# Two state-space layers on one core: where layer 1's near part and tail put their loads, sums and roots

## The chip, the cores and the metric

One core of one Trainium2 chip. Its engines are TensorE (PE: matmuls), VectorE (DVE), ScalarE (ACT), GpSimd (POOL) and SyncE (SP). Each takes its own instructions in order, and they wait for one another by semaphores. TensorE writes to PSUM, the other on-chip memory is SBUF. Transfers between these and the main memory are issued by SP, ScalarE or GpSimd, each on a queue of its own, and carried by 16 DMA engines that all queues share. The metric is the device time of one launch in microseconds (us), the median of several runs.

## The reference, cut to what matters

An image of 64 x 64 tokens with 96 channels goes through two layers of the same build: group norm, projection to 192 channels and as many gates, depthwise 3x3 convolution, four scans along rows and columns in both directions, layer norm, gating, projection back, and the sum with the input.

```python
# one layer (both have these steps; what differs is the form of the scan)
xz = gn(x) @ in_proj_w
xin, z = split(xz)
u = silu(depthwise_conv3x3(xin) + conv_b)
dt = softplus((u @ x_proj)[:6] @ dt_proj + bias)   # B, C: 16 states each
# per channel and state n, along each of four orders of the tokens
h[t] = h[t-1] * exp(dt[t] * A[n]) + dt[t] * u[t] * B[t, n]
y[t] = sum_n h[t, n] * C[t, n] + u[t] * D
y = layernorm(y1 + y2 + y3 + y4) * g + b
x = x + (y * silu(z)) @ out_proj_w
```

Layer 1 computes its scan as `decay * cumsum(dB_u / (decay + 1e-12))`: once the decay has fallen far enough under 1e-12, a state gives nothing any more. So all that its scans give lies near their starts. Layer 2's scans are true recurrences over all 4,096 tokens.

## The kernel before

Channels lie on partitions: 192 channels as three blocks T = 0, 1, 2 of 64, each block with the two halves of the image on partitions 0 to 63 and 64 to 127, so that a tensor like `u[T]` or `y[T]` is 128 x 2048. A chunk c (0 to 3) is 512 of these columns. Many operations are recorded by one helper, so that their line in the profile is L271 (the class `Ordered`, which keeps an engine's instructions in the order of the program) or L805 (the same within layer 2's scans); the names of their tiles tell them apart.

Layer l runs: `head` (norm of the group, projection `in`, convolution with `pad`, gates `sz` stored to `szd`), the scans, `tail` or `last_tail`.

**Layer 1's near part, `near_scans`.** Only the first 192 steps of each of four directions are computed, and fewer for the states that decay faster: `kinds` holds (192, state pair 0), (64, pair 1), (32, pairs 2 to 7). `us` is the input of the scans, 128 x 3 x 2 x 384; `dt`, `du` and `S` (the running sum of dt) have that shape too. `steps_of(T)` copies dt (ScalarE), forms du = dt times us (VectorE), sends both across the two halves of the partitions by SP (`across`) and forms the sums (VectorE). `sums_of(T)` copies the sums to `S` and sends them across. B and C, 16 rows each, are stored to main memory (`stored`) and fetched again with every row spread over 64 partitions (`fetched`). The work is cut into six units j: `operands(j)` gives the decays a, `weights_of(j)` a weight `wt` from `S` by Tanh, `inputs(j)` B times du (GpSimd), `scan(j)` the weighting product `nbw` and the scan `nnh` on VectorE and the product with C, `nnhc`, on GpSimd; `add(j)` sums over states in PSUM by matmul. `mean` and `centre` take the mean over channels off y. The order of all this is written out by hand at the end of the function; `look_ahead()` in it loads layer 2's small weights and the half p=1 of its scan weights. The function returns a flag that tells whether the near steps were enough; every engine reads it and branches over the full form (`far_scans`), which doesn't run with these inputs.

**Scan weights, `scan_weights(l, p, queue)`.** For layer 2 they are 44 loads for one p: 11 each for two directions and two halves. Before, the half p=0 is loaded by the loop over layers, on SP's queue as it is, not in the hand-written order: a scheduler places the loads where their tiles are free.

**Layer 1's tail, `tail`.** It works by chunk from 3 down to 0. `squares` (ScalarE), `variance` (matmuls with a matrix of means), `root` (Ln, then Exp with -0.5), then the gating y * root * gain + bias times the gate: blocks 0 and 1 on VectorE (`gated`, two instructions), block 2 on GpSimd and ScalarE (`pool_gated`); `project` (12 matmul records a chunk), `add` (sum with x and statistics for layer 2's norm, VectorE; a write to `xs` by SP, which only the last tail reads). `load_exp_ln()` asks for a ScalarE table that holds both Exp and Ln.

Then layer 2's `head` begins with the aggregation `gst` of the statistics, a norm with Ln and Exp, and the projections `in`; `borders(b)` copies, by SP, the border rows between the parts of `pad`, which the taps of the upper and lower row of the convolution need. Its first scan step needs the half p=0 of the scan weights.

The part of the hand-written orders that the change touches:

```python
            steps_of(0)
            inputs(0)
            inputs(1)
            steps_of(1)
            cb += [fetched("C", rows, i) for i in range(1, len(kinds))]
            sums_of(0)
            mean(3)
...
            load_exp_ln()
            squares(3)
            variance(3)
            squares(2)
            root(3)
```

Of the kernel before, what the change touches and what calls it, by code (L numbers as in the profile page):

```python
# [21 lines left out]
NS = 16  # L22
# [22 lines left out]
def two_ss2d_layers(  # L45
# [231 lines left out]
    def near_scans(weights, ds):  # L277
# [5 lines left out]
        with ExitStack() as sc:  # L283
# [42 lines left out]

            us = once.tile([128, 3, 2, 2 * NEAR], F32, name="nus")
            k = NEAR // HW
# [45 lines left out]
            def fetched(what, kept, i):  # L374

                n, m0, m1 = kinds[i]
                t = once.tile([128, m1 - m0, 4, n], F32, name=f"n{what}b{n}")
                for h, half in enumerate(HALF):
                    if n in kept:
                        to, of = t[half], kept[n][2 * m0 + h : 2 * m1 : 2]  # L380
                    else:
                        to, of = t[half, 0], kept[NEAR][2 * m0 + h, :, 0:n]
                    sp.dma_start(out=to, in_=of.unsqueeze(0).to_broadcast(to.shape))
                return t.rearrange("p n d w -> p (n d w)")

            rows = stored("B", 0)
            B = [fetched("B", rows, i) for i in range(len(kinds))]
            rows = stored("C", NC - NS)
            cb = [fetched("C", rows, 0)]

# [16 lines left out]
            for i, (n, m0, m1) in enumerate(kinds):  # L407
# [4 lines left out]
            )  # L412
            dt, du, S = (
                once.tile([128, 3, 2, 2 * NEAR], F32, name=f"n{nm}") for nm in ("dt", "du", "S")
            )
# [69 lines left out]
            def operands(j):  # L485
                T, ks = units[j]
                long = sum(4 * kinds[i][0] * (kinds[i][2] - kinds[i][1]) for i in ks)
                a, wt, h, hc = live[j] = [
                    nb.tile([128, 1024], F32, tag=nm, name=f"n{nm}{j}")[:, 0:long]
                    for nm in ("na", "nwt", "nh", "nhc")  # L490
                ]
# [126 lines left out]
            steps_of(0)  # L618
            inputs(0)
            inputs(1)  # L620
            steps_of(1)
            cb += [fetched("C", rows, i) for i in range(1, len(kinds))]
            sums_of(0)
            mean(3)
# [910 lines left out]
    def tail(l, w, xT):  # L1535
# [3 lines left out]
        with ExitStack() as sc:  # L1539
# [26 lines left out]
            def root(c):  # L1566
                r = live["r", c] = fin.tile([128, HT], F32, tag="rstd", name=f"rstd{l}_{c}")
                act.activation(r, live.pop(("v", c)), AF.Ln, bias=eps5)
                act.activation(r, r, AF.Exp, scale=-0.5)

# [4 lines left out]
            def gated(c, T):  # L1575
                q, gain, bias = result(c, T)
                dve.scalar_tensor_tensor(
                    q, y[T][:, at(c)], gain, live["r", c], ALU.mult, ALU.mult
                )
                dve.scalar_tensor_tensor(q, q, bias, sz[c, T], ALU.add, ALU.mult)  # L1580

            def pool_gated(c, T):
                q, gain, bias = result(c, T)
                pool.tensor_mul(q, y[T][:, at(c)], live["r", c])
                act.activation(q, q, AF.Identity, bias=bias, scale=gain)
# [11 lines left out]
            def add(c):  # L1597
                po = live.pop(("o", c))
                for h in range(2):
# [3 lines left out]
                    sp.dma_start(out=xs[:, at(g)], in_=xT[:, at(g)])  # L1603

            load_exp_ln()
            squares(3)
            variance(3)
            squares(2)
            root(3)
            for c in order:  # L1610
# [3 lines left out]
                for T in (0, 1):  # L1614
                    gated(c, T)
                if c > 1:
                    squares(c - 2)
                if c:
                    root(c - 1)
                project(c)  # L1620
# [171 lines left out]
    def look_ahead():  # L1792
        ahead["w"] = layer_weights(1, sp)
        ahead["sw"] = scan_weights(1, 1, sp)

    for l in range(2):

        w = ahead.pop("w") if l else layer_weights(0, nc.sync)
        sw = list(zip(*[scan_weights(l, 0, nc.sync)] + ([ahead.pop("sw")] if l else [])))

# [103 lines left out]
```

## Time and profile before

| what | value |
|---|---|
| median of 3 runs | 1483.68 us (1482.44 to 1490.68) |
| profiled execution | 1493.08 us, its span 1491.1 us |
| instructions | 17293 |
| busy share of the span | DVE 90%, ACT 83%, PE 82%, POOL 82% |
| granted TensorE clock | 0.922 of full |

The page's 40 slices are 37.3 us each. Digits are busy tenths of an engine in a slice:

```profile
PE   5864668788888888888887989888889898887988
DVE  5848578688999998999999999999998999999996
ACT  5755547789889978999999999999997999897873
POOL 2715228779989897999898989898989898989895
PEclk9986789589999989999999999999998999999999
```

Slices 3 to 6, roughly 75 to 224 us, are the near part, the tail and the start of layer 2: there no engine is near full. From about slice 8 on layer 2's scans keep VectorE nearly full up to the last slice.

In the timeline used below each line has the start in us from the span's start, the length, engine, line, operation with output and inputs, and in brackets the idle time just before and what ended it. SPq is SP issuing a transfer. In groups, the columns are operation and shapes with the count, busy us and mean ns of one, and the idle time before them by releaser.

### The profile page before, as it was taken

How to read it: one execution, taken by the hardware profiler on the slowest of the kernel's cores; microseconds unless marked ns; L12 is line 12 of the kernel's file. 1: busy time of each engine (PE TensorE's matmuls, PEld its weight loads, DVE VectorE, ACT ScalarE, POOL GpSimd, SP SyncE). 2: the span in 40 equal slices, each digit the busy share in tenths (PEclk: the TensorE clock that was granted, in tenths of full speed). 3: DMA queues.
4: the chain of work that ended last, by engine and by line, in shares of the span. 5: the costliest groups of instructions: out<-in, count | busy, mean ns of one | idle time of the engine just before them, and what ended most of it. 6: DMA issues, size and time to landing. Idle time of an engine off the chain costs nothing.

```text
span 1491.1 us, 17293 instructions
## 1 busy us (share of the span) xinstructions
PE 1225.7 (82%) x5019; PEld 471.8 (32%) x5019; DVE 1338.8 (90%) x920; ACT 1234.6 (83%) x2524; POOL 1220.4 (82%) x678
## 2 busy tenths in 40 slices
PE   5864668788888888888887989888889898887988
PEld 2233213333332323233333333333333332322333
DVE  5848578688999998999999999999998999999996
ACT  5755547789889978999999999999997999897873
POOL 2715228779989897999898989898989898989895
PEclk9986789589999989999999999999998999999999
DMA  3241522515252625262626262626262626262634
GB/s 106 73 120 30 141 50 84 140 45 137 63 133 63 149 57 128 62 149 62 153 60 145 57 143 58 142 58 142 59 141 59 142 59 147 62 146 62 151 84 129
DMA packets 87475, 148.65 MB, mean 100 GB/s; under 512 B 34572, under 2 KB 38476, under 8 KB 87276
## 3 DMA queue, kind: packets, MB, share of 16 engines
q1 hardware_dynamic: 85692, 144.92, 40.4%
q0 software_dynamic: 576, 1.57, 0.5%
q10 hardware_dynamic: 1104, 0.98, 0.2%
q8 instruction: 40, 0.66, 0.2%
q14 instruction: 63, 0.52, 0.1%
HBM read 81.77 MB, written 12.17 MB: 63 GB/s over the span
## 4 chain that ended last, share of the span: by engine, by line
DVE 23%; issue 19%; PE 14%; ACT 13%; POOL 8%; DMA 8%; SPq 5%; DVEq 0%; POOLq 0%; ACTq 0%
DVE h L805 15%; DVE b L805 6%; POOL hc L805 5%; DMA cb<-C 4%; ACT a L805 4%; PE pj L805 4%; SPq L805 3%; ACT bT L805 3%; PE ys L805 3%; PE b L805 2%; DMA dt<-sp 2%; DMA szt<-szd 1%; POOL sp L805 1%; PE cp L271 1%; POOL ln L805 1%
## 5 line engine op out<-in xcount | busy, mean ns | idle before, releaser
L805 POOL TENSOR_TENSOR hc<-h,cb 128x1024 f32<-128x1024 f32 x384 | 903.2, 2372 | 104.3 <-DVE h L805 54.1
L805 DVE TENSOR_TENSOR_SCAN h<-a,carry,b 128x1024 f32<-128x1024 f32 x288 | 665.1, 2338 | 30.3 <-PE b L805 6.8
L805 ACT ACTIVATE a<-dt,am 128x1024 f32<-128x1024 f32 x384 | 438.2, 1141 | 57.7 <-DVE h L805 54.7
L805 PE MATMUL ys<-hc,fold 128*64 128x512 f32 x1536 | 434.0, 645 | 0.6 <-POOL hc L805 0.5
L805 ACT ACTIVATE bT<-duT,BT 128x192 f32<-128x192 f32 x1012 | 387.0, 445 | 3.1 <-PE b L805 0.9
L805 PE MATMUL b<-ident,bT 128*128 128x128 f32 x1536 | 226.0, 291 | 25.3 <-DVE h L805 19.4
L805 DVE TENSOR_TENSOR b<-b,du 128x1024 f32<-128x1024 f32 x192 | 232.1, 1209 | 11.4 <-PE b L805 11.4
L805 DVE TENSOR_TENSOR_SCAN h<-a,b 128x1024 f32<-128x1024 f32 x96 | 216.2, 2278 | 12.3 <-PE b L805 4.3
L805 PEld LDWEIGHTS b<-ident,bT 128*128 128x128 f32 x1536 | 179.2, 148 | 151.3 <-DVE h L805 89.1
L805 PE MATMUL b<-B,selh 96*128 96x512 bf16 x384 | 118.8, 392 | 124.3 <-DVE h L805 123.9
L805 PEld LDWEIGHTS ys<-hc,fold 128*64 128x64 f32 x1536 | 78.4, 139 | 144.9 <-issue 112.4
L805 PEld LDWEIGHTS <-selh 96*128 96x128 bf16 x384 | 26.2, 99 | 253.8 <-DVE h L805 197.9
L805 PE MATMUL pj<-u,xw 64*124 64x512 f32 x192 | 101.4, 677 | 1.7 <-DVE w L805 1.2
L271 POOL TENSOR_TENSOR tap<-tap,tap 128x512 f32<-128x512 f32 x48 | 60.9, 1273 | 49.2 <-ACT tap L271 46.6
L271 DVE SCALAR_TENSOR_TENSOR acc<-pad,v,acc 128x1052 f32<-128x1052 f32 (+1 forms) x64 | 75.2, 1182 | 2.1
L805 ACT CAST B<-pj 96x512 bf16<-96x512 f32 (+2 forms) x96 | 54.9, 575 | 8.4 <-PE pj L805 8.4
L805 PE MATMUL ys<-y,ident 128*128 128x512 f32 (+1 forms) x120 | 61.0, 610 | 0.0
L805 POOL TENSOR_TENSOR sp<-sp,ln 128x512 f32<-128x512 f32 x45 | 57.8, 1284 | 0.2
L805 POOL TENSOR_TENSOR ln<-ln,w 128x512 f32<-128x512 f32 x45 | 57.8, 1284 | 0.0
L805 POOL TENSOR_TENSOR su<-sp,u 128x512 f32<-128x512 f32 x45 | 57.7, 1281 | 0.0
L805 PEld LDWEIGHTS pj<-u,xw 64*124 64x124 f32 x192 | 35.6, 200 | 62.8 <-issue 49.5
L805 PE MATMUL pd<-xd,dwb 29*64 29x512 f32 x192 | 54.5, 640 | 0.0
(189 smaller groups left out, 1210.6 us busy)
## 6 DMA issues: line engine op xcount, KB each, us to landing
cb<-C SPq DMA_DIRECT2D x256, 256.0 KB, 4.1
dt<-sp SPq DMA_DIRECT2D x192, 128.0 KB, 4.5
du<-su SPq DMA_DIRECT2D x180, 128.0 KB, 4.0
szd<-sz SPq DMA_DIRECT2D x24, 256.0 KB, 2.0
szt<-szd SPq DMA_DIRECT2D x24, 256.0 KB, 8.3
xT<-xs SPq DMA_DIRECT2D x8, 384.0 KB
xs<-xT SPq DMA_DIRECT2D x1, 1536.0 KB
xs<-xT SPq DMA_DIRECT2D x8, 192.0 KB, 2.4
```

The lines of the kernel that those rows point to most:

```text
L271: return lambda *args, **more: tc.keep_in_program_order(op(*args, **more))
L805: return lambda *args, **more: tc.keep_in_program_order(op(*args, **more))
```

## The change

- The half p=0 of layer 2's scan weights is no longer loaded by the loop over layers but by `look_further()`, called first in the tail's order, on SP in the order written.
- Rows of C are stored right behind those of B, and all six fetches of C are issued by GpSimd instead of SP.
- `S` takes the place of `us` in SBUF (one tile for both), and the decays and weights `na`, `nwt` get three buffers instead of two.
- `sums_of(0)` comes ahead of `inputs(1)` and `steps_of(1)`.
- In the tail the root is written to PSUM (`r`) and, by one more Exp, to SBUF (`low`, for GpSimd); the half product of `gated` goes to PSUM (`q`). `r` and `q` have one buffer each.
- In the tail the table load stands behind the squares of chunk 3, `root(3)` ahead of `squares(2)`, and in the loop `root(c - 1)` ahead of `squares(c - 2)`.

```diff
@@ -324,7 +324,7 @@
                         y[T][:, s], u[T][:, s], ds[:, T : T + 1], ps, ALU.mult, ALU.subtract
                     )
 
-            us = once.tile([128, 3, 2, 2 * NEAR], F32, name="nus")
+            us = S = once.tile([128, 3, 2, 2 * NEAR], F32, name="nus")
             k = NEAR // HW
             
             for T in range(3):
@@ -380,13 +380,15 @@
                         to, of = t[half], kept[n][2 * m0 + h : 2 * m1 : 2]
                     else:
                         to, of = t[half, 0], kept[NEAR][2 * m0 + h, :, 0:n]
-                    sp.dma_start(out=to, in_=of.unsqueeze(0).to_broadcast(to.shape))
+                    (sp if what == "B" else pool).dma_start(
+                        out=to, in_=of.unsqueeze(0).to_broadcast(to.shape)
+                    )
                 return t.rearrange("p n d w -> p (n d w)")
 
             rows = stored("B", 0)
+            more = stored("C", NC - NS)
             B = [fetched("B", rows, i) for i in range(len(kinds))]
-            rows = stored("C", NC - NS)
-            cb = [fetched("C", rows, 0)]
+            cb = [fetched("C", more, i) for i in range(len(kinds))]
 
             pd = []
             for T in range(3):
@@ -410,8 +412,8 @@
                 once.tile([128, 3, 2 * NEAR], F32, name=f"n{nm}")
                 for nm in ("w", "ln", "t", "v", "sums")
             )
-            dt, du, S = (
-                once.tile([128, 3, 2, 2 * NEAR], F32, name=f"n{nm}") for nm in ("dt", "du", "S")
+            dt, du = (
+                once.tile([128, 3, 2, 2 * NEAR], F32, name=f"n{nm}") for nm in ("dt", "du")
             )
             for T in range(3):
                 act.activation(w[:, T], pd[T], AF.Abs)
@@ -486,8 +488,8 @@
                 T, ks = units[j]
                 long = sum(4 * kinds[i][0] * (kinds[i][2] - kinds[i][1]) for i in ks)
                 a, wt, h, hc = live[j] = [
-                    nb.tile([128, 1024], F32, tag=nm, name=f"n{nm}{j}")[:, 0:long]
-                    for nm in ("na", "nwt", "nh", "nhc")
+                    nb.tile([128, 1024], F32, tag=nm, name=f"n{nm}{j}", bufs=n)[:, 0:long]
+                    for nm, n in (("na", 3), ("nwt", 3), ("nh", 2), ("nhc", 2))
                 ]
                 for n, m, s in states(j):
                     act.activation(
@@ -617,10 +619,9 @@
 
             steps_of(0)
             inputs(0)
+            sums_of(0)
             inputs(1)
             steps_of(1)
-            cb += [fetched("C", rows, i) for i in range(1, len(kinds))]
-            sums_of(0)
             mean(3)
             mean(2)
             steps_of(2)
@@ -1564,24 +1565,27 @@
                     pe.matmul(pv, pos, live.pop(("sq", c, T)), start=(T == 0), stop=(T == 2))
 
             def root(c):
-                r = live["r", c] = fin.tile([128, HT], F32, tag="rstd", name=f"rstd{l}_{c}")
-                act.activation(r, live.pop(("v", c)), AF.Ln, bias=eps5)
-                act.activation(r, r, AF.Exp, scale=-0.5)
+                low = live["low", c] = fin.tile([128, HT], F32, tag="low", name=f"low{l}_{c}")
+                r = live["r", c] = fps.tile([128, HT], F32, tag="r", name=f"r{l}_{c}", bufs=1)
+                act.activation(low, live.pop(("v", c)), AF.Ln, bias=eps5)
+                act.activation(r, low, AF.Exp, scale=-0.5)
+                act.activation(low, low, AF.Exp, scale=-0.5)
 
             def result(c, T):
                 q = live["g", c, T] = fin.tile([128, HT], F32, tag=f"g{T}", name=f"g{l}_{c}_{T}")
                 return q, v[:, T, V_G : V_G + 1], v[:, T, V_B : V_B + 1]
 
             def gated(c, T):
-                q, gain, bias = result(c, T)
+                g, gain, bias = result(c, T)
+                q = fps.tile([128, HT], F32, tag="q", name=f"q{l}_{c}_{T}", bufs=1)
                 dve.scalar_tensor_tensor(
                     q, y[T][:, at(c)], gain, live["r", c], ALU.mult, ALU.mult
                 )
-                dve.scalar_tensor_tensor(q, q, bias, sz[c, T], ALU.add, ALU.mult)
+                dve.scalar_tensor_tensor(g, q, bias, sz[c, T], ALU.add, ALU.mult)
 
             def pool_gated(c, T):
                 q, gain, bias = result(c, T)
-                pool.tensor_mul(q, y[T][:, at(c)], live["r", c])
+                pool.tensor_mul(q, y[T][:, at(c)], live["low", c])
                 act.activation(q, q, AF.Identity, bias=bias, scale=gain)
                 pool.tensor_mul(q, q, sz[c, T])
 
@@ -1602,21 +1606,22 @@
                     dve.bn_stats(w["next"][:, g, :], xT[:, at(g)])
                     sp.dma_start(out=xs[:, at(g)], in_=xT[:, at(g)])
 
+            look_further()
+            squares(3)
             load_exp_ln()
-            squares(3)
             variance(3)
+            root(3)
             squares(2)
-            root(3)
             for c in order:
                 if c:
                     variance(c - 1)
                 pool_gated(c, 2)
                 for T in (0, 1):
                     gated(c, T)
+                if c:
+                    root(c - 1)
                 if c > 1:
                     squares(c - 2)
-                if c:
-                    root(c - 1)
                 project(c)
                 if c < NCH - 1:
                     add(c + 1)
@@ -1791,12 +1796,15 @@
 
     def look_ahead():
         ahead["w"] = layer_weights(1, sp)
-        ahead["sw"] = scan_weights(1, 1, sp)
+        ahead["sw"] = [scan_weights(1, 1, sp)]
+
+    def look_further():
+        ahead["sw"] = [scan_weights(1, 0, sp)] + ahead["sw"]
 
     for l in range(2):
 
         w = ahead.pop("w") if l else layer_weights(0, nc.sync)
-        sw = list(zip(*[scan_weights(l, 0, nc.sync)] + ([ahead.pop("sw")] if l else [])))
+        sw = list(zip(*(ahead.pop("sw") if l else [scan_weights(0, 0, nc.sync)])))
 
         later = head(l, ones, w)
         xp.close()
```

## The prediction

> **What bounds the kernel now.** I read the 40 slices of the page first, then the chain that ended last in order of time, then the timeline and the groups of the first 210 us, then the DMA queue's waits. The scans of layer 2 fill the span from about 260 us to 1476 us, and no line of the diff touches their instructions. So the change lives in two stretches: the near part of layer 1 (88 to 156 us) and layer 1's tail with the start of layer 2 (158 to 209 us). Its worth is what these two get shorter.
>
> Near part, timeline (start, length, engine, line, operation, in brackets the idle time before it and its releaser):
>
> ```profile
> 97.59 1.04 ACT L271 COPY nS<-nsums 64x384 f32<-64x384 f32 x2 [0.37 <-DVE nsums L271]
> ...
> 101.51 3.35 DVE L271 SCALAR_TENSOR_TENSOR y<-u,ds,nm 128x512 f32<-128x512 f32 x5
> ...
> 103.22 2.61 SPq L271 DMA_DIRECT2D nCb<-nC  x4
> ...
> 105.94 1.21 SPq L271 DMA_DIRECT2D nS<-nS  x2
> ...
> 109.96 1.03 ACT L271 ACTIVATE nnwt<-nS,lneps,am 128x768 f32<-128x768 f32 x1 [6.25 <-DMA nS<-nS]
> ...
> 111.09 0.97 DVE L271 SCALAR_TENSOR_TENSOR nbw<-nnwt,nb 128x768 f32<-128x768 f32 x1 [6.23 <-ACT nnwt L271]
> ```
>
> The sums of T=0 lie ready at 98.6, but their transfer is issued at 105.9, because SP's queue holds dt, du and four fetches of C ahead of it. VectorE has done all else at 104.86 and stands still for 6.23 us.
>
> Tail, timeline, then groups of the same window (busy us, mean ns, idle before):
>
> ```profile
> 165.32 0.69 ACT L271 ACTIVATE rstd<-v,eps 128x512 f32<-128x512 f32 x1 [1.36 <-PE v L271]
> ...
> 166.02 1.28 ACT L271 ACT_TABLE_LOAD   x1
> ...
> 167.32 0.63 ACT L271 ACTIVATE rstd<-rstd 128x512 f32<-128x512 f32 x1
> ```
>
> ```profile
> L271 ACT ACT_TABLE_LOAD x10 | 12.8, 1283 | 20.5 <-DVEq L1811 20.3
> L271 DVE SCALAR_TENSOR_TENSOR g<-y,v,rstd 128x512 f32<-128x512 f32 x8 | 10.2, 1276 | 12.4 <-ACT rstd L271 12.4
> L271 DVE SCALAR_TENSOR_TENSOR g<-g,v,szt 128x512 f32<-128x512 f32 x8 | 8.8, 1106 | 0.3
> ```
>
> Each root has a table load ahead of its Ln and another ahead of its Exp, and VectorE waits 12.4 us for roots. The gating starts of the four chunks are at 167.98, 176.24, 183.93 and 191.60: a period of 7.8 us. ScalarE fills it: wait for GpSimd's first product 1.3, affine 0.82, squares 1.65, load, Ln, load, Exp 1.28+0.69+1.28+0.63, sum 7.65. ScalarE is the pace of the tail. Gating in layer 2's tail has root and half product in PSUM already, and shows what it costs there:
>
> ```profile
> L271 DVE SCALAR_TENSOR_TENSOR q<-y,v,r x8: 743/756/756, 1460.7 to 1474.4; 128x512 f32<-128x512 f32 x8
> L271 DVE SCALAR_TENSOR_TENSOR g<-q,v,szt x8: 743/751/752, 1462.3 to 1475.8; 128x512 f32<-128x512 f32 x8
> ```
>
> **What the Trainium skill says.** "SBUF — State Buffer", section "Who interferes with whom": a VectorE instruction with two SBUF inputs contends with a GpSimd instruction that reads SBUF, and with at most one it doesn't. The trace agrees: 1276 and 1106 ns in layer 1's tail against 756 and 751 in layer 2's. "ScalarE: Activation LUTs", section "What ACT_TABLE_LOAD costs": 1283 ns plus a drain of about 1380. The trace has the 1283; Ln ends at 166.01 and the load starts at 166.02, so of the drain nothing is seen, and I price a load at 1.3. "TensorE: Matmul & The Clock Gate", section "What's actually happening": half clock after idle windows of about 3.4 us, full after as long a busy one. The trace agrees roughly: a variance matmul record takes 0.86 us until 164.5 and 0.43 from 165.1, five us after the array started.
>
> **The change part by part.** Near part. SP loses, ahead of the near transfers, the loads of ab (seven between 85 and 97 us) and six fetches of C (3.7 us), and the sums of T=0 move ahead of T=1. ScalarE then does dt of T=0 to 96.15, the sums copies 97.59 to 98.63 (VectorE's sums end at 97.56), four dt copies to 100.75, na(0) to 101.69, S copies of T=1 to 102.73. SP issues S of T=0 at 98.2 and 98.75; at the 2.1 to 3.6 us that nS takes to land it is there at 102.3 at the latest, so nnwt(0) runs 102.75 to 103.8. The first weighting product can start when VectorE is free, at 104.9: 6.2 earlier. Next late: ds, whose reduction now stands right behind the first scan and waits for v of layer 2, and centre(1), which waits for the mean matmuls. These start at 104.92 as before, since they need VectorE's five centre operations done; six records of 0.85 end at 110.1. v is issued at 107.65 (SP: six more pairs after S of T=0, then ipw) and lands 2.25 later, at 109.9. So VectorE goes on at 110.1 instead of 113.83 and does ds 0.17, centre(1) 2.04, the second product 1.25 (before 2.02, beside GpSimd's product; GpSimd is idle from 111.4) and its scan 2.29: done at 115.9 instead of 121.45. From there on the order and the neighbours are those of before. **Gain 5.6**; the bounds are 3 (the second product and a landing stay slow) and 6.5 (the whole wait and a little contention).
>
> GpSimd gets the six fetches of C. The nearest row is its issue of du in layer 2, 0.52 us each (12 issues, landing 3.0 to 9.5 us). They run from about 89.5, when C has landed, to 93 at that price and to 96 at 1 us each. Its queue's next work is nb(0), which waits for du until 100.3; nb(0) and nb(1) then end at 104.7, and the first product needs only nb(0) at 102.2. C is needed first at 107.7. So they are hidden with some 4 us to spare; without that cover each us of theirs is one of VectorE. Three buffers of a and wt take away ScalarE's waits of 2.7 us for scans, but ScalarE is off the path there: nothing. S in place of us: S is written after VectorE's products of the same T in any case: nothing.
>
> Tail. Let t0 be the first ScalarE instruction after the branch (158.14 before, 152.5 after). In the built order of the changed kernel there is one table load in the tail, between the squares of chunk 3 and its Ln; ten (and the one ahead of the branch) go, the one between Ln and Exp of layer 2's norm among them. Each root gains one Exp of 0.63. Step by step:
> - Squares start at t0 instead of t0+1.3, and the load lies behind the variance matmuls: these run t0+0.7 to 5.9 (six records of 0.86, half clock). Ln 0.69, Exp into r 0.63: r(3) at 7.25 (before 9.83). Gain 2.6.
> - Second Exp to 7.9, squares(2) to 9.5. variance(2) 8.6 to about 11.6 (0.43 to 0.6 a record), r(2) at 13.0 (before 18.1).
> - From here the longest of three loops is the period. ScalarE 0.69+0.63+0.63+1.62+0.82 = 4.4 and its waits; VectorE four at 0.75 and add with statistics, four at 0.68: 5.8; TensorE variance 6 x 0.43 and projection 12 x 0.28: 5.9 at full clock. The loop root, squares, variance takes 0.7+0.65+0.65+0.55+2.6 = 5.2 and then queues behind the projection. I take 6.3 a chunk, TensorE not being at full clock throughout: r(1) 19.5, r(0) 25.8.
> - VectorE gates chunk 0 to 28.8, add(1) to 31.5; projection(0) waits for GpSimd's block (second Exp 26.4, product 1.3, affine 0.82, product 1.4: 29.9) and ends at 31.2; add(0) to 34.3. With a half us of small waits (q and r have one buffer each: a wait of VectorE for itself under 0.1 each) the aggregation of the statistics starts at t0+35.3, before at 202.12, t0+44.0. **Gain 8.7**, bounds 4.5 and 10.5.
> - Norm of layer 2: no load between Ln and Exp, **gain 1.3**.
>
> Layer 2's first weights: 44 loads are now together on SP, after the tail's own loads and ahead of the eight writes of xs and of the border rows of pad. SP ends the tail's loads at t0+13.9 as before. The same 44 for the other half of layer 2 took 27.3 us (115.88 to 143.15). With 2 us for lanes that wait for the big loads: t0+43.2; eight writes at 0.55: 47.6; the first four border transfers to 50, landing 2.2 later at 51 to 52. VectorE needs the first of them 19 us after the aggregation (before 221.1 against 202.12), less 1.3: t0+53. So hidden, by 1 to 2 us only. Before, the same queue was free at about 208.5, t0+50.4. The weights themselves are needed at 259.9. **Cost 0**, bounds 0 and 5.
>
> Sum: 5.6 + 8.7 + 1.3 = 15.6. The profiled execution took 1493.08 (span 1491.1 and 2.0 around it), so it would go to 1477.5; the median of before is 9.4 lower, 1483.68, and gives **1468.1**.
>
> **The rivals.**
> - TensorE sets the pace in the tail. For: its clock was 0.5 in 172 to 178 and 196 to 198, and gaps remain. Against: less waiting elsewhere keeps it busier. The period stays 7.8; then the tail gains the 2.6 of the start and about 1.7 of contention in the last chunk: 5.6+4.3+1.3 = 11.2, 1472.5. Chance 0.15.
> - C on GpSimd's queue comes late or holds up nb(0). For: landing of GpSimd's transfers is 7.3 in the median against 4 for SP's, and C meets B on the engines. Against: 8 us until it is needed. The near gain is lost, 10.0 remain: 1473.7. Chance 0.08.
> - SP is late for layer 2's borders. For: the spare time above is small, and everything before it gets earlier while SP does not. At 0.75 us a load instead of 0.62 the border lands 5.7 later, a stall of 4.3: 1472.4. This one has the other sign too: each load past 0.62 costs 44 times that, less 1.5 spare; at 1.02 us a load the whole 15.6 is eaten, and at 1.2 the stall is 24 and the time 1492. Against: no load of this kind was issued in over 0.7 in the trace. Chance 0.11, of which 0.04 over the sign.
> - That the table loads stay is excluded by the built order.
>
> **How the numbers follow.** Forecast 0.66, rivals 0.15, 0.08, 0.11. The forecast's own bounds, with the parts not all at one end, are a gain of 10.5 to 19.5: 1464 to 1473; executions of before spread over 8 us, so I widen to 1461 and, to take in the first two rivals, 1476. A measurement of this kernel tells about 0.5%, 7.4 us, from no change: a gain under that has the low ends of the forecast and the rivals, 0.07; slower 0.04; faster 0.89.
>
> **What would show it.** nnwt(0) no longer waits for nS and the first product starts near 105; the end of the near part, hence the branch, is 5 to 6 earlier. In the tail one table load, both gating forms at 0.75, starts of gating 6 to 7 apart, aggregation 35 to 36 after t0. SP's first border transfer is issued at t0+47 to 49, and VectorE's border taps don't wait for pad. From the first projection of layer 2's scans on, all is as before, shifted by about 15.6. Wrong it would be if VectorE waits for pad in layer 2's convolution, if GpSimd's nb(0) starts after 103, or if the roots still come 7.8 apart with TensorE at half clock.

## The result and the profile after

The changed kernel takes 1472.9 us in the median (1467.99 to 1482.94) against 1482.43 (1478.26 to 1490.68) for the kernel before, 14 runs each: ratio 0.9936, 95% interval 0.9915 to 0.9958, a gain of 9.5 us (6.2 to 12.6). The forecast was 1468.1. Its direction and its range held; 6 of the expected 15.6 us are missing in the medians.

The profiled executions can't be set against each other as they are: 1493.08 us at a granted clock of 0.922 before, 1467.99 at 0.940 after. So the spans are cut at the same instructions in both, and each stage is compared by itself. Times are from the span's start:

| stage, from its start to its end | before | after | gain |
|---|---|---|---|
| near part, to the first ScalarE instruction after the branch (t0) | 158.14 | 154.28 | 3.86 |
| tail, from t0 to the aggregation `gst` | 43.98 | 34.53 | 9.45 |
| norm, from `gst` to the first product `in` of layer 2 | 6.65 | 5.31 | 1.34 |
| layer 2's head, to the first x projection `pj` of its scans | 51.09 | 51.35 | -0.26 |
| from `pj` to the first exponential `a` | 15.88 | 18.78 | -2.90 |
| from that to the first scan `h` | 10.88 | 10.49 | 0.39 |
| sum up to the first scan of layer 2 | 286.62 | 274.74 | 11.88 |
| the rest, all scans of layer 2 and the last tail | 1204.5 | 1191.5 | 13.0 |

Up to layer 2's first product nearly all of the forecast is there (14.65 of 15.6 us). Then 2.9 us are given back within 16, in a place where the diff has no line. Two figures say how finely such stages can be read. The kernel before, profiled again, has t0 at 157.40 instead of 158.14. And the changed tail takes 33.0 to 34.5 us from t0 to `gst` in the nine other kernels of this study that keep its table load and its use of PSUM; most of that difference lies in the first six variance matmuls, 4.27 us in the shortest and 5.49 here.

Near part, timeline of the changed kernel:

```profile
98.11 1.19 SPq L271 DMA_DIRECT2D nus<-nus  x2
...
102.61 1.03 ACT L271 ACTIVATE nnwt<-nus,lneps,am 128x768 f32<-128x768 f32 x1
...
104.70 1.82 DVE L271 SCALAR_TENSOR_TENSOR nbw<-nnwt,nb 128x768 f32<-128x768 f32 x1
...
104.84 7.55 PE L271 MATMUL nm<-u,average 128*128 128x512 f32 x12 [11.76 <-DVE y L271]
...
110.57 0.17 DVE L237 TENSOR_REDUCE ds<-v 128x3 f32<-128x12 f32 x1 [2.18 <-DMA v<-in_vec_dram]
...
112.43 2.06 DVE L271 SCALAR_TENSOR_TENSOR y<-u,ds,nm 128x512 f32<-128x512 f32 x3 [1.70 <-PE nm L271]
```

The sums of T=0 leave at 98.11 instead of 105.94, so `nnwt` doesn't wait and the first product `nbw` starts at 104.70 instead of 111.09: the stall of 6.23 us is gone. Two new ones stand behind it: 2.18 us for `v` of layer 2, and 1.70 for the mean matmuls. The last line starts at 112.43, when the matmul group ends (104.84 + 7.55 = 112.39, all twelve records). The group itself starts only at 104.84, when all of VectorE's earlier centre operations, those on both chunks that held the tile before, are done.

Tail, timeline:

```profile
154.28 1.67 ACT L271 ACTIVATE sq<-y 128x512 f32<-128x512 f32 x3 [26.63 <-DVEq L1819]
...
155.96 1.28 ACT L85 ACT_TABLE_LOAD   x1
...
160.49 0.69 ACT L271 ACTIVATE low<-v,eps 128x512 f32<-128x512 f32 x1 [3.24 <-PE v L271]
161.20 0.60 ACT L271 ACTIVATE r<-low 128x512 f32<-128x512 f32 x1
161.84 0.63 ACT L271 ACTIVATE low<-low 128x512 f32<-128x512 f32 x1
161.84 0.76 DVE L271 SCALAR_TENSOR_TENSOR q<-y,v,r 128x512 f32<-128x512 f32 x1 [6.69 <-ACT r L271]
```

The only table load lies inside the wait for the variance matmuls. The four chunks' gating starts at 161.84, 168.97, 174.70 and 180.35, so 7.1, 5.7 and 5.65 us apart instead of 8.3, 7.7 and 7.7. Groups of the tail (busy us, mean ns, idle before):

```profile
L271 DVE SCALAR_TENSOR_TENSOR q<-y,v,r 128x512 f32<-128x512 f32 x8 | 6.0, 751 | 10.8 <-ACT r L271 10.7
L271 DVE SCALAR_TENSOR_TENSOR g<-q,v,szt 128x512 f32<-128x512 f32 x8 | 6.0, 751 | 0.3
...
L85 ACT ACT_TABLE_LOAD x1 | 1.3, 1283 | 0.0
```

Both gating forms cost 0.75 us. SP and the borders, timeline:

```profile
198.66 4.50 SPq L271 DMA_DIRECT2D xs<-xT  x8
...
203.33 12.49 SPq L271 DMA_DIRECT2D pad<-pad  x12
...
203.79 18.74 DVE L271 SCALAR_TENSOR_TENSOR acc<-pad,v,acc 128x1052 f32<-128x1052 f32 x14
```

The first border leaves at t0+49.05, and VectorE's row of 14 taps has no wait in front of it.

The place where time is given back, timeline of the kernel before and then of the changed one:

```profile
269.85 0.69 DVE L805 SCALAR_TENSOR_TENSOR sp<-pd,wl 128x512 f32<-128x512 f32 x1
...
270.64 2.40 SPq L805 DMA_DIRECT2D dt<-sp  x4
...
272.41 2.26 POOL L805 DMA_DIRECT2D du<-su  x4
...
273.14 1.21 SPq L805 DMA_DIRECT2D cb<-C  x2
...
274.91 2.61 SPq L805 DMA_DIRECT2D dt<-sp  x4
...
275.74 1.15 ACT L805 ACTIVATE a<-dt,am 128x1024 f32<-128x1024 f32 x1 [1.28 <-DMA dt<-sp]
```

```profile
255.47 0.69 DVE L806 SCALAR_TENSOR_TENSOR sp<-pd,wl 128x512 f32<-128x512 f32 x1
...
256.58 2.41 SPq L806 DMA_DIRECT2D dt<-sp  x4
...
258.02 2.10 POOL L806 DMA_DIRECT2D du<-su  x4
...
259.09 1.27 SPq L806 DMA_DIRECT2D cb<-C  x2
...
260.52 4.19 SPq L806 DMA_DIRECT2D dt<-sp  x4
...
264.25 1.15 ACT L806 ACTIVATE a<-dt,am 128x1024 f32<-128x1024 f32 x1 [4.18 <-DVE su L806]
```

The four issues of `dt` take the same time in both. The exponential that needs them starts 2.7 us after the last issue has ended before (273.04 to 275.74), 5.3 after (258.99 to 264.25). VectorE is named as the releaser of the 4.18 us, but only because its `su` of the last block ends 0.2 us ahead; before, the exponential doesn't wait for that `su`.

The traces also hold the times at which each transfer counts up its completion semaphore; no line above prints them. By these, three of the four `dt` transfers land almost as before, and the fourth alone is late. In us after the start of `pj`: 13.0, 13.6, 14.3 and 15.8 before; 13.4, 14.0, 14.7 and 18.6 after. The exponential starts at 15.9 and 18.8.

A second difference is small but visible in the lines. SP begins the first `dt` 0.10 us after `sp` is ready before (270.54 to 270.64) and 0.42 us after it in the changed kernel (256.16 to 256.58). GpSimd's first `du` leaves 12.55 us after `pj` in both. So the fourth `dt` is issued within 0.03 us of it before, and 0.37 us behind it after. The completion semaphores on SP are eight, taken in turn (101 to 108 in the traces, counted 0 to 7 below).

### The profile page after: what moved, and what is told of

It is laid out like the page before. It is cut to its first block, busy times and chain, and to the rows that moved or that the text cites. A ratio compares the mean times of both kernels' runs of the same rounds, so it can differ in the third digit from the quotient of the medians.

```text
span 1466.2 us, 17295 instructions
## 1 busy us (share of the span) xinstructions
PE 1195.6 (82%) x5019; PEld 461.4 (31%) x5019; DVE 1331.0 (91%) x920; ACT 1222.5 (83%) x2517; POOL 1222.4 (83%) x684
## 4 chain that ended last, share of the span: by engine, by line
DVE 28%; issue 23%; POOL 10%; ACT 10%; PE 9%; DMA 7%; SPq 2%; DVEq 0%; POOLq 0%; ACTq 0%
DVE h L806 18%; DVE b L806 8%; POOL hc L806 7%; DMA cb<-C 4%; ACT a L806 3%; ACT bT L806 2%; PE ys L806 2%; SPq L806 2%; PE pj L806 1%; PE b L806 1%; POOL sp L806 1%; DMA xT<-xs 1%; DMA du<-su 1%; POOL ln L806 1%; PE cp L271 1%
## 5 line engine op out<-in xcount | busy, mean ns | idle before, releaser
L806 PE MATMUL ys<-hc,fold 128*64 128x512 f32 x1536 | 429.5, 638 | 0.5 <-POOL hc L806 0.5
L806 PE MATMUL b<-ident,bT 128*128 128x128 f32 x1536 | 220.0, 286 | 28.9 <-DVE h L806 21.0
L806 PEld LDWEIGHTS b<-ident,bT 128*128 128x128 f32 x1536 | 174.4, 145 | 151.3 <-DVE h L806 90.4
L806 PEld LDWEIGHTS <-selh 96*128 96x128 bf16 x384 | 25.8, 97 | 257.1 <-DVE h L806 201.0
L806 PE MATMUL pj<-u,xw 64*124 64x512 f32 x192 | 91.5, 621 | 1.9 <-DVE w L806 1.2
```

Of the source, the lines that this page charges most:

```text
L806: return lambda *args, **more: tc.keep_in_program_order(op(*args, **more))
```

## The experiments

Theory of the near part: the wait for all twelve mean records comes from the one PSUM tile that the means of two chunks share, and costs the missing 1.7 us. Rival: VectorE is held by the late reduction of ds in any case. Theory of the tail: the table loads are most of the gain (about 6 us), PSUM for root and half product the smaller part. Rival: the reverse. For the time given back: a side effect of where the weights, or C, now stand in the queues, or chance.

All experiments but the last two have one time each, and executions of one kernel spread over some 10 us; what they tell is read from their stages.

**Mean tiles of their own.**

```diff
-                if c % 2:
-                    live["mean"] = pps.tile([128, 2, 512], F32, tag="B", name=f"nm{c}")
-                ps = live["mean", c] = live["mean"][:, c % 2]
+                t = pps.tile([128, 2, 512], F32, tag="jB"[c % 2], name=f"nm{c}")
+                ps = live["mean", c] = t[:, 0]
```

> The changed kernel, with the means of each chunk in a PSUM tile of their own. In the profile of the changed kernel VectorE stood for 2.18 us for layer 2's v and then 1.70 us more for the mean matmuls, until all twelve records had ended. Theory A: the second wait comes from the two chunks sharing one tile, so centre(1) can start only when both are done; then it starts right behind ds, near 110.8 instead of 112.4, and the branch (first ScalarE instruction behind it, 154.28 there) comes 1.5 to 2 us earlier. Rival B: the mean matmuls of chunk 1 alone are not done sooner at half clock; then the branch does not move.

Measured: with this edit the scheduler also moved the reduction of ds back behind the second scan, and centre(1) started at 108.86, directly behind the first scan, without a wait. t0 is 152.43, 1.85 earlier than in the changed kernel, although the near part's first product came 1.1 later in this run (105.84); from that product on the near part is 3.0 shorter. The time was 1472.82. Both waits are gone here, so the run doesn't say what the tile alone is worth.

**The same, and ds reduced in the tail.**

```diff
-        nc.vector.reduce_sum(w["ds"], v[:, :, V_D : V_D + 4], axis=AX.X)
+        if l == 0:
+            sum_d(nc.vector, w)
...
     def look_further():
+        sum_d(dve, ahead["w"])
         ahead["sw"] = [scan_weights(1, 0, sp)] + ahead["sw"]
```

> The same with the reduction of ds for layer 2 put into the tail, so that no VectorE instruction of the near part waits for v. Theory A: nothing is left between the first scan's end (108.4) and centre(1); the second product starts near 110.5 instead of 114.4, partly beside GpSimd, and the branch comes 3 to 4 us earlier than 154.28. Rival B (the matmuls set it): 0 to 0.5 us. Rival C (GpSimd's products become the next limit of the near part): 1.5 to 2 us, no more than in the run with the means alone.

Near part of this kernel, timeline:

```profile
94.40 4.54 PE L275 MATMUL nm<-u,average 128*128 128x512 f32 x6 [1.94 <-DVE y L275]
...
102.89 5.49 PE L275 MATMUL nm<-u,average 128*128 128x512 f32 x6 [3.96 <-DVE y L275]
...
103.12 0.97 DVE L275 SCALAR_TENSOR_TENSOR nbw<-nnwt,nb 128x768 f32<-128x768 f32 x1 [0.28 <-ACT nnwt L275]
...
107.50 2.04 DVE L275 SCALAR_TENSOR_TENSOR y<-u,ds,nm 128x512 f32<-128x512 f32 x3
...
109.46 1.23 DVE L275 SCALAR_TENSOR_TENSOR nbw<-nnwt,nb 128x1024 f32<-128x1024 f32 x1
```

The twelve records have become two groups of six. The first, chunk 1's, starts at 94.40, as soon as centre(3) has freed its tile, ten us earlier than in the changed kernel, and is long done when centre(1) needs it. The second, at 102.89, is chunk 0's and still runs when centre(1) starts at 107.50 without a wait, where the changed kernel has 112.43. So the shared tile did two things: it let the means start only when both chunks before were centred, and it made centre(1) wait for both. t0 is 149.20, 5.1 earlier than in the changed kernel where 3 to 4 were expected; 1.6 of it is there at the first product, which comes at 103.12 in this run. The first scan is at 268.21, 6.5 earlier, the rest of that lying in the tail, which this edit hardly touches. The time was 1465.32. That the wait for twelve records came from the tile is shown; the wait for `v` was removed beside it in both runs, so the two are not priced apart.

**The table load ahead of the squares.**

```diff
             look_further()
-            squares(3)
             load_exp_ln()
+            squares(3)
             variance(3)
```

> The changed kernel with the table load asked for ahead of the squares again, all else as changed. Built, this has a load ahead of the branch and ten in the tail. Theory T (the loads are most of the tail's gain): the load on each root's way returns, gating starts 6.9 to 7.8 apart instead of 5.6, aggregation of the statistics at t0+40 to 43 instead of t0+34.5, and 1.3 more between it and the first projection of layer 2. Rival P (PSUM for root and half product is what counts): aggregation at t0+35 to 37.

Tail of this kernel, timeline and then a group:

```profile
161.13 0.69 ACT L271 ACTIVATE low<-v,eps 128x512 f32<-128x512 f32 x1 [2.73 <-PE v L271]
161.84 1.28 ACT L271 ACT_TABLE_LOAD   x1
163.13 0.60 ACT L271 ACTIVATE r<-low 128x512 f32<-128x512 f32 x1
```

```profile
L271 ACT ACT_TABLE_LOAD x10 | 12.8, 1283 | 25.6 <-DVEq L1819 25.4
```

One line moved by one place, and the loads are all back, one ahead of each Ln and one ahead of each Exp. The first ScalarE instruction after the branch starts at 154.14, the aggregation at 195.28, t0+41.1 against 34.5 (40 to 43 expected), though its gatings start 9.4, 6.8 and 6.8 us apart and not 6.9 to 7.8; the norm takes 6.57 us again. So the loads' place is worth 6.6 us in the tail and 1.3 in the norm. The Trainium skill, "ScalarE: Activation LUTs", section "What ACT_TABLE_LOAD costs", adds a drain of about 1380 ns to each load of 1283; here Ln ends at 161.82 and the load starts at 161.84, and the Exp starts as the load ends: no drain is seen.

**Root and half product in SBUF.**

```diff
-                r = live["r", c] = fps.tile([128, HT], F32, tag="r", name=f"r{l}_{c}", bufs=1)
+                r = live["r", c] = fin.tile([128, HT], F32, tag="r", name=f"r{l}_{c}")
...
-                q = fps.tile([128, HT], F32, tag="q", name=f"q{l}_{c}_{T}", bufs=1)
+                q = g
```

> The changed kernel with the root and the half product in SBUF, all else as changed (the second Exp stays). Theory T: VectorE's two gating forms go back from 0.75 to a mean of 1.1 to 1.3, but TensorE and ScalarE set the pace; aggregation at t0+35 to 36.5. Rival P: VectorE, near 5.7 us a chunk without contention, goes to 7.3 and sets the pace; aggregation at t0+38 to 41.

Groups of its tail:

```profile
L271 DVE SCALAR_TENSOR_TENSOR g<-g,v,szt 128x512 f32<-128x512 f32 x8 | 10.7, 1339 | 0.3
L271 DVE SCALAR_TENSOR_TENSOR g<-y,v,r 128x512 f32<-128x512 f32 x8 | 6.9, 866 | 9.0 <-ACT r L271 9.0
```

1339 and 866 ns against 751 and 751, that is 16 instructions for 17.6 us instead of 12.0. The Trainium skill's "SBUF — State Buffer", section "Who interferes with whom", says that a VectorE instruction with two SBUF inputs contends with a GpSimd instruction that reads SBUF, and this agrees. Of the 5.6 us 3.3 reach the aggregation (t0+37.86 against 34.53), between the two expectations and near the second. The two parts, 6.6 and 3.3, come to 9.9 beside the 9.45 that the tail gained, so the loads are the larger part. The order of roots and squares, and the Exp that was added, were not undone by themselves; what they give is at most the small difference.

**C on SP again, and layer 2's first weights in the near part again**, each alone and then together.

```diff
-                    (sp if what == "B" else pool).dma_start(
+                    sp.dma_start(
```

```diff
-            look_further()
             squares(3)
...
-        sw = list(zip(*(ahead.pop("sw") if l else [scan_weights(0, 0, nc.sync)])))
+        sw = list(zip(*[scan_weights(l, 0, nc.sync)] + (ahead.pop("sw") if l else [])))
```

> The changed kernel with C fetched by SP again (six fetches of some 0.5 us each move back from GpSimd's queue to SP's, ahead of layer 1's first scans). If GpSimd's queue is worth something in the near part, the branch's first squares, 154.3 us in the changed kernel, come 1 to 4 us later; if C was hidden on either queue, they stay within 0.5 us of 154.3. Start of layer 2's scans: the changed kernels took 18.7 to 18.9 us from layer 2's first x projection to the first exponential of its scans, where the kernel before took 15.9. SP's DMA semaphores go round in turn, and six fetches less on SP shift every later transfer of SP by six places. If that shift (or C's place on GpSimd's queue) is what makes the first dt transfers land late, this kernel goes back to 15.9; if the weights' new place is, it stays at 18.7 to 18.9.

> The changed kernel with layer 2's first weights loaded where the kernel before loaded them (by the loop over the layers, in the near part), all else as changed. If the late loading does anything for the near part, SP has 44 loads more ahead there and the branch's first squares come after 154.3 us (1 to 3 us); if SP had room, they stay within 0.5. On the other side SP is free for the borders, which wait for nothing in the changed kernel either: no gain there. Start of layer 2's scans: 15.9 us from the first x projection to the first exponential if the late weights are what delays the first dt transfers, 18.7 to 18.9 if C on GpSimd or the shift of SP's semaphores is.

> The changed kernel with both taken back: C on SP and layer 2's first weights loaded by the loop over the layers in the near part. What is left there of the change is the order (sums of T=0 right behind the inputs of T=0), the buffers and the shared tile. With C alone back the first squares came at 154.02, with the weights alone back at 154.44, against 154.28. If each of the two is enough by itself, taking both back brings 2 us or more (156 to 158); if the order alone made the near part's gain, it stays within 0.8 of 154.3. Start of layer 2's scans 15.9 to 16.8 us as with C back.

Measured: t0 at 154.02 with C back, 154.44 with the weights back, 155.18 with both, against 154.28. The last is 0.1 beyond its band, but there only ScalarE's wait at the branch is longer (28.44 us, 26.63 in the changed kernel); VectorE's third product stands at 120.57 (121.48 in the changed kernel) and the first gating at 161.61 (161.84). So for C, GpSimd's queue brings nothing to the near part over SP's at the same early place.

More can't be read from these three, because they don't restore the queue of the kernel before. With C on SP its six fetches still stand right behind B's (91.72 to 95.61 with both back), ahead of `dt`; in the kernel before, four of them stood at 103.22, directly ahead of the sums. And with the weights in the loop again the scheduler put one of their `ab` loads ahead of the near transfers, not the seven of before; most of the others came at 137 and later. What is left for the near part's 3.9 us is the new order as a whole: sums of T=0 ahead of T=1, C's fetches moved up, the `ab` loads gone. Its parts, the third buffers and the shared tile were not tried one by one.

The other reading is the time from `pj` to the first exponential: 16.75 us with C back, 16.73 with both, 18.88 with the weights back alone. The weights' place in the order has no part in the time given back; C's move has, though 16.75 is neither of the two values that were expected. Times of one run each: 1477.27, 1480.39, 1469.43.

**The kernel before once more.**

> The kernel before once more with a profile. If the start of layer 2's scans is a property of the kernel, the first x projection to the first exponential takes 15.9 us again, and the branch's first squares come at 158.1; if it varies from run to run, it comes out somewhere between 15.9 and 18.9. The rest, from the first scan to the end, took 1204.5 us at a mean clock of 0.922 and 1191.5 in the changed kernel at 0.940: if the clock makes that difference, this run stands on the same line (about 7 us for each 0.01 of clock).

15.86 us from `pj` to the exponential (15.88 in the first profile): a property of the kernel, not of the run. The squares' place did not repeat as well, with t0 at 157.40 instead of 158.1. The rest from the first scan took 1198.1 at a clock of 0.936, some 6 us less than at 0.922, where 7 us for each 0.01 would have made it 10.

**Six and three small transfers more on SP.** C's six fetches that left SP shift all later transfers of SP by six places in the turn of eight completion semaphores. These two kernels put transfers of 32 bytes, read by nothing, on SP beside C's fetches:

```diff
                     (sp if what == "B" else pool).dma_start(
                         out=to, in_=of.unsqueeze(0).to_broadcast(to.shape)
                     )
+                    if what == "C":
+                        sp.dma_start(out=spare_row[:, i, h], in_=dtw[0, 0:1, 0, 0:8])
```

(for three: `if what == "C" and h:`)

> The changed kernel, C still fetched by GpSimd's queue, but with six transfers of 32 bytes on SP in the places where C's fetches were. SP's later transfers then use the same semaphores as in the kernel before (the first dt transfer of layer 2's scans has number 5 of 8 there and 7 in the changed kernel), while GpSimd's queue keeps its six transfers more. From layer 2's first x projection to the first exponential of its scans: about 16 to 17 us if SP's turn of semaphores is what matters (15.9 before, 16.75 with C back on SP), 18.7 to 18.9 if it is GpSimd's turn or anything else of C's new place. The branch's first squares stay within 0.8 us of 154.3.

> The changed kernel with three transfers of 32 bytes on SP instead of six. The first dt transfer of layer 2's scans then has semaphore 2 of 8, where it has 5 in the kernel before and 7 in the changed one. If the turn of SP's semaphores sets how soon these transfers land, the first x projection to the first exponential comes out somewhere of its own, between 15.5 and 19.5 us; if it is only the time that the six transfers take on SP or in the near part, it is half way, about 17.4.

Start of the scans with six more, timeline:

```profile
254.91 2.40 SPq L809 DMA_DIRECT2D dt<-sp  x4
...
257.41 1.64 SPq L809 DMA_DIRECT2D cb<-C  x2
...
259.23 2.88 SPq L809 DMA_DIRECT2D dt<-sp  x4
...
260.17 1.15 ACT L809 ACTIVATE a<-dt,am 128x1024 f32<-128x1024 f32 x1 [1.39 <-DMA dt<-sp]
```

`pj` starts at 244.16, so it is 16.01 us, and the wait for `dt` is 1.39 instead of 4.18: 2.8 of the 2.9 us come back with C still on GpSimd's queue. With three more it is 15.86, not half way. (t0 is 153.34 with six more, just outside the 0.8 us expected.) Times of one run each: 1468.75 and 1474.84, at clocks of 0.936 and 0.925. Over all the runs, with the semaphore of the first `dt` and the landing of the fourth read from the traces (times in us after `pj`):

| semaphore | C fetched by | first `dt` issued | fourth `dt` landed | exponential | kernels |
|---|---|---|---|---|---|
| 7 | GpSimd | 11.11 to 11.12 | 18.5 to 18.7 | 18.69 to 18.88 | the changed one, and the five experiments that left its SP queue at this count |
| 5 | GpSimd | 10.75 | 15.8, 15.9 | 15.91, 16.01 | six more, and six more with the near part's repairs (below) |
| 2 | GpSimd | 10.75 | 15.8 | 15.86 | three more |
| 5 | SP | 10.78 | 15.8 | 15.86, 15.88 | the kernel before, twice |
| 5 | SP | 11.11 to 11.12 | 16.6 to 16.7 | 16.69 to 16.75 | C back in the changed kernel, three kernels |

So the place in the turn is not all. The last two rows have the same semaphore; what differs is that SP issues the first `dt` a third of a us later, and the fourth lands 0.8 later. The rest, nearly 2 us, separates the first row from the last, at the same moment of issue. No kernel has place 7 with an early issue, or place 5 with a late one and C on GpSimd, so the turn of semaphores and the moment of issue, which both change with the small transfers, are not told apart.

The engines' traffic at that place, in stretches of 2 us from the first `dt` issue on (busy us of the five, clock, DMA share, GB/s), the third stretch in the changed kernel and then with six more:

```profile
260.60:262.60 2.00, 0.00 (x0) 0.00 (x0) 1.91 (x3) 0.00 (x0) 1.09 (x3) 0.50 0.94 183
```

```profile
258.90:260.90 2.00, 0.00 (x0) 0.00 (x0) 1.93 (x4) 0.73 (x1) 0.68 (x2) 0.50 1.03 265
```

The DMA engines are nearly as busy, but move 183 instead of 265 GB/s just when the fourth `dt` should land. What is shown is that, with C on GpSimd's queue, the number of transfers that SP has issued before decides the landing; C's place on that queue does not by itself. How it does that (by the semaphores, by SP's short delay, or by which transfer is served first beside `du` of GpSimd and `cb` from main memory) these runs don't show.

**The best version.** The edits above put together: mean tiles of their own and ds in the tail, once with C on SP, once with C on GpSimd and six transfers more.

> The changed kernel with mean tiles of its own for each chunk and the reduction of ds in the tail (as in the run before that had both), and C fetched by SP as in the kernel before. Expected from the stages: branch's first squares at about 149.2 (154.3 changed), layer 2's first x projection to the first exponential 16.0 to 16.8 us (18.8 changed), first scan of layer 2 at 265.5 to 266.5 (274.7 changed, 286.6 before). If that carries to the end, the time is some 8 us under the changed kernel's 1472.9 and the ratio to the kernel before 0.986 (0.983 to 0.989); if what is gained ahead of the scans is lost in them, the ratio stays at the changed kernel's 0.9936. If C on SP, in front of the sums, is late for the now earlier near part, the squares come at 150 to 152.

> The same two repairs of the near part, with C on GpSimd's queue as in the changed kernel and six transfers of 32 bytes on SP that bring its semaphores to the turn of the kernel before. Squares at 149.2, x projection to first exponential 16.0 us, first scan at 265 to 266. Ratio to the kernel before 0.986 (0.983 to 0.989), the same as with C on SP or up to 0.8 us better; 0.9936 if the scans take the gain back.

Beside 1481.1 (12 runs) of the kernel before: with C on SP 1467.15 (7 runs), ratio 0.9905 (0.9873 to 0.9938), a smaller gain than expected; with six more 1462.39 (6 runs), ratio 0.9873 (0.9835 to 0.9910), as expected. The two intervals overlap. From `pj` to the exponential both did as expected (16.69 and 15.91). The first scans, at 267.00 and 268.44, are later than expected in both, and t0 is 149.69 in the first but 152.07 in the second. There the first twelve mean matmuls take 7.11 us, where the other kernel has 5.42; VectorE waits 1.73 us for the first of them, and the first product comes at 106.42 instead of 103.21.

The last version is the fastest of all by its median, 10.5 us under the changed kernel's; it has not been timed side by side with that. Its six runs had a mean granted clock of 0.940, the kernel before 0.933 beside them, so by the table at the end of the next section some 4 of its 18.7 us may go with the clock.

## Why the prediction was right in direction and short in size

- **Near part, 5.6 forecast, 3.86 measured.** That the first product would start at 104.9 held (104.70), and so, nearly, did the landing of `v` (110.6 against 109.9). The step that failed is "six records of 0.85 end at 110.1. [...] So VectorE goes on at 110.1": centre(1) waited for the end of all twelve records, 112.4, because both chunks' means lie in one PSUM tile. With tiles apart the wait is gone. That t0 then came at 152.43, beside the forecast's 152.5, is luck: in that run the first product was 1.1 later than forecast, and centre(1) started at 108.86, with no wait for ds either. The first product's 1.82 us, beside GpSimd's product, cost nothing in the changed kernel: VectorE then waited for `v` anyway.
- **Weights and C.** "SP loses, ahead of the near transfers, the loads of ab [...] and six fetches of C" is the forecast's account of why the sums leave earlier, together with their new place. They do leave at 98.11 (98.2 forecast). Which of these moves is needed stays open, since no run put the loads and C's four late fetches back where they were. That C is hidden on GpSimd's queue (rival at 0.08) held: six issues of 0.64 us from 89.69, and nothing waits for C.
- **Tail, 8.7 forecast, 9.45 measured**, inside its bounds, and in part by errors that cancel. r(3) came at t0+7.5 (7.25 forecast), but r(2) at t0+14.7 instead of 13.0: its variance matmuls ran mostly at half clock (0.50 granted from 164 to 166), 4.54 us for six records where the forecast had 3. The next two periods, 5.7 and 5.65, were shorter than the 6.3 assumed, TensorE being at full clock from the projection of chunk 3 on, so that r(0) came at 25.7 beside 25.8. The forecast's last step also adds up to t0+34.8, not the 35.3 that it gives (34.3 and half a us of small waits); measured 34.5. The rival of TensorE setting a pace of 7.8 fell; only the first period, 7.1, has something of it.
- **Norm, 1.3 forecast, 1.34 measured.**
- **SP and the borders, 0 forecast, 0 measured.** First border at t0+49.05, at the top of the forecast's t0+47 to 49; VectorE doesn't wait. This rival fell too.
- **"From the first projection of layer 2's scans on, all is as before"** failed: 2.9 us go there. The mistake was to see in the move of C six issues on two queues, and not that everything SP issues later has another number of transfers ahead of it. No price for that stood in the sum; measured, the fourth `dt` lands 2.8 us later than before.
- **What remains.** 15.6 - 1.7 (near part) - 2.9 (landing of `dt`) + 0.75 (tail) comes to 11.75, and 11.88 is what the traces show up to the first scan. The medians' 9.5 has an interval up to 12.6, so this agrees; the 2.4 us between them have no cause shown. The rest of the span is no evidence: it lies between 1191.2 and 1204.5 us over the profiles of all kernels of this study, and it goes with the granted clock more than with the kernel:

| granted clock | rest from the first scan to the end, us |
|---|---|
| 0.922, 0.925 | 1204.5, 1201.8 |
| 0.928 to 0.931 | 1201.1, 1199.4, 1203.6 |
| 0.934, 0.935 | 1199.5, 1202.5 |
| 0.936 | 1198.1, 1195.3, 1195.9 |
| 0.938 to 0.940 | 1197.7, 1195.2, 1191.5 |
| 0.944 | 1191.2 |

## What to carry to other kernels

When a stall is taken away, look at what the next instruction waits for by tile, not by instruction. Here two results in one PSUM tile were waited for together, and the tile could be filled again only when both had been read. A transfer moved to another queue changes what is ahead of all that follow on the old one, so look at the landing of the next critical transfers, one by one, even if they are far away. A few idle transfers show whether the count matters. They change more than one thing at once, so they don't yet tell why. When an edit is taken back, read in the trace where the moved transfers stand now: a scheduler or a hand-written order may have put them in a third place. A table load that the program places itself is worth trying on both sides of the first function that needs another table: one place further up, the compiler put nine more into the tail and one into the norm.

## What the runs showed of the hardware that was not expected

- Of four `dt` transfers, issued alike within 2.4 us, the last landed 18.5 to 18.7 us after `pj` in six profiles, 16.6 to 16.7 in three and 15.8 to 15.9 in five. With C on GpSimd's queue the number of transfers that SP had issued long before decides between late and early; through which of the things that change with it is open. The three in the middle have C on SP, and the same number as the kernel before.
- Over 14 profiles the stage of layer 2's scans gets about 6 us shorter for each 0.01 of granted clock, although VectorE, not TensorE, is the fullest engine there (95% and 85% busy in the changed kernel). This is a correlation, with single profiles up to 5 us off the line; nothing was done to the clock.
- The same twelve mean matmuls at 87 us took 5.42 us in nine of the profiles and 7.11 in five. With the shared tile this left the first product where it was (104.31 and 104.42 in two of the slow cases, 103.75 to 104.70 in the others of the changed kernel's order); with tiles apart, where VectorE takes up the first chunk's mean earlier, it came some 3 us later (105.84 and 106.42 against 103.12 and 103.21). So a single profile doesn't fix a near part to better than that; only intervals between its own instructions can be compared.
